# Turning the second pass over a layer's end chunks around, keeping their taps, and leaving GpSimd's products out of eight iterations

## The chip, the cores and the metric

The kernel runs on one core of a Trainium2 chip. The metric is the device time in microseconds (us) of one execution. The kernel before has a median of 3023.64 us in 3 runs (3022.08 to 3026.47).

## What is computed

Four layers work on an image batch x of 4 x 32 x 32 x 16 (batch, rows, columns, channels). Each of the first three normalises x by groups and computes, for every output position ij of the 32 x 32, a 3 x 3 convolution of the whole image with taps of its own, a rectifier of the difference to the image, and a weighted sum over the image:

```
first = jnp.einsum('ijpq,bpqc->bijc', M2, inputs)
K = jnp.transpose(G, (2, 3, 4, 0, 1, 5)).reshape(kh, kw, c, h * w * f)
shifted = lax.conv_general_dilated(inputs, K, window_strides=(1, 1), padding='SAME', ...)
diff = jax.nn.relu(inputs[:, :, :, None, None, :] - shifted)
second = jnp.einsum('ijpq,bpqijc->bijc', W2, diff)
return first - L * second          # and x = x + that
```

The fourth layer is a filter whose impulse response comes from a quotient of transforms. The change doesn't touch its code.

## The kernel before, in words

**Blocks and iterations.** A layer's 1024 positions times 16 channels are 128 blks of 128 rows. One iteration (`iteration`) takes one blk and one batch: TensorE (PE) convolves the whole image (1024 pixels) with the blk's taps into PSUM. Batches 0 and 2 go through `direct` (L637, 10 matmul records in an iteration), batches 1 and 3 through `shared` (L656 and L676, 22 records), which computes part of the sum once for two pixels. ScalarE (ACT) copies that part out of PSUM (L664), and VectorE (DVE) adds it (L684). Then the result is clipped at zero, multiplied by the weights W of the blk and summed over the pixels. DVE does that in one instruction (L725), or ACT clips it into SBUF (L705), GpSimd (POOL) multiplies (L706, here "a product"), and ACT sums (L711). Which way is taken, `by_pool` decides.

**Chunks and their tiles.** Four blks are a chunk; chunks are numbered through the three layers, 32 in each. A chunk needs three things:
- four of the taps, a tile f of 512 KB, loaded by `load_f` (L497) on SyncE's queue (SP) and corrected by one POOL instruction (`minus_mid`, L489). Three buffers in turn.
- the other taps, a tile g. `other_taps` prepares them once for each chunk: it loads E on SP (L525), then POOL makes two sums and a split of them in steps (L489, L530, L534, L536) and stores the pieces to DRAM (gd, L539). `beside_products` spreads the steps over iterations without a product. `piece_loads` fetches them with a broadcast in two DMAs of 768 KB on SP (g<-gd, L554), once the store is noted. Two buffers in turn.
- W for two blks, 1 MB, loaded by `w_loads` on SP (L601). Six buffers in turn.

**The order.** In each layer five jobs follow each other. Job 0 takes the first 12 blks for one pair of batches, job 1 the same 12 blks for the other pair, job 2 the middle 104 blks for all four batches, jobs 3 and 4 the last 12 blks for pair (0, 1), then for pair (2, 3). A pair job has 24 iterations, job 2 has 416. The pairs are (0, 2) and (1, 3) in layer 0, so job 1 there is `shared` alone, and (0, 1) and (2, 3) after it. So a pair's sums are complete while the other pair still has 24 iterations to go, and its next image can be made beside these. Each of jobs 0, 1, 3 and 4 goes through its three chunks from the lowest up, so each chunk is loaded for each pair.

**Behind a pair's end.** `conv_layer` adds the pair's sums to x on DVE (L764) and starts `make_image`: group norm (statistics on DVE, L150 to L180, sums over partitions by PE, L130), centring and scaling (L332, L1077 in the last layer), then `store_image` (pieces on ACT, POOL and DVE, then img<-ys and img<-ye on SP) and `load_image` (f<-img and n<-img, half on SP and half on POOL). PE, DVE, ACT, POOL and SP each work strictly through the order in which the program issued to them.

**Who sets the order.** It is written out by the program itself: a counter now["at"] counts iterations, and every load is a generator that waits for a count. `step` advances them all after each iteration. F of a use u is due at begin[u] - 30, or when use u - 2 begins; g of a use at begin[u] - 12, or when use u - 1 begins, which is eight iterations ahead in a pair job. E of a chunk is planned backwards from that (`ready`: 20 iterations earlier, 14 apart) and forwards through `done`; the very first chunk to be prepared may start at iteration 3, others 8 behind their load. W waits while an image is being stored and loaded (now["image"]).

Of the kernel before, what the change touches and what calls it, by code (L numbers as in the profile page):

```python
# [15 lines left out]
P = 128  # L16
B, C, S = 4, 16, 32
NBLK = 128
# [19 lines left out]
def conv_stack_kernel(ctx, tc, x, M, W, first_w, first_f, first_g, F, E, h0, coef, cst, dft, idp, idq, out):  # L38
# [4 lines left out]
    work = ctx.enter_context(tc.tile_pool(name="work", bufs=1))  # L43
    small = ctx.enter_context(tc.tile_pool(name="small", bufs=2))
    imp = ctx.enter_context(tc.tile_pool(name="image", bufs=1))
    wp = ctx.enter_context(tc.tile_pool(name="wp", bufs=6))
    gs = ctx.enter_context(tc.tile_pool(name="gs", bufs=3))
    gn = ctx.enter_context(tc.tile_pool(name="gn", bufs=2))
    ge = ctx.enter_context(tc.tile_pool(name="ge", bufs=1))
    er = ctx.enter_context(tc.tile_pool(name="er", bufs=2))  # L50
    rp = ctx.enter_context(tc.tile_pool(name="rp", bufs=2))
# [39 lines left out]
    for layer in range(3):  # L91
        firsts = [FIRST, tuple(b for b in range(B) if b not in FIRST)] if layer == 0 else [(0, 1), (2, 3)]
        blks = start[layer]
        passes += [(blks[0], pair) for pair in firsts] + [(blks[1], (0, 1, 2, 3))]
        passes += [(blks[2], pair) for pair in ((0, 1), (2, 3))]
    order, uses, w_first, w_last = [], [], {}, {}
    for blks, batches in passes:
        for blk in blks:
            if blk % GC == 0:
                uses.append([blk // GC, len(order), any(SHARED[b] for b in batches)])  # L100
            w_first.setdefault(blk // 2, len(order))
            order += [(blk, b, len(uses) - 1) for b in batches]
            w_last[blk // 2] = len(order)
    begin = [use[1] for use in uses] + [len(order)]
    now = {"at": 0, "image": 0}

    def until(at):
        while now["at"] < at:
            yield
# [81 lines left out]

    def first_images(nine, g9):

        gn0 = taps_tile().rearrange("p d u s n -> p (d u s n)")
        for u in range(3):
            gt[u] = gn0[:, bass.ts(u, GC * P)]
        rlo = st.tile([P, B], F32, name="rlo")
        ims_of = lambda b: ims[0, b]

# [26 lines left out]

        def first_lo(u, r):
            part = g9[u]
            lo = gt[u][r : r + 32]
            nc.vector.tensor_tensor(lo, part[r : r + 32], lo.bitcast(F32), ALU.subtract)  # L230

        def first_taps(u):
            nc.scalar.copy(gt[u], g9[u])

        all_sums = []

# [196 lines left out]
    def first_term(layer, xt):  # L433

        ft = work.tile([P, 2, 8, S], F32, tag="ft", name="ft")
        with tc.tile_pool(name="mp", bufs=4) as mp:
            mts = [load_m(mp.tile([P, 2 * 512], F32, tag="mt", name="mt"), layer, 0)]
            yield

            yt = work.tile([P, 8, B, C], F32, tag="yt", name="yt")  # L440
            for b in range(B):
                nc.vector.transpose(yt[:, :, b, :], yc[b // 2][:, b % 2, :])
            for pm in range(1, 4):
                mts.append(load_m(mp.tile([P, 2 * 512], F32, tag="mt", name="mt"), layer, pm))
                yield

            for pm in range(4, 8):
                if pm % 2 == 0:
                    while not w_free():
                        yield  # L450
                    wt = w_tile(None)
                mts.append(load_m(wt[:, pm % 2], layer, pm))
                yield
            for _ in range(4):
                yield
            pf = small_psum()
            for k, mt in enumerate(mts):
                for h in range(2):
                    nc.tensor.matmul(  # L459
                        pf[64 * h : 64 * h + 64],  # L460
                        lhsT=yt[:, k].rearrange("k b c -> k (b c)"),
                        rhs=mt[:, bass.ts(h, 512)],
                        start=(k == 0),
                        stop=(k == len(mts) - 1),
                    )
            ring[:] = [last or now["at"] for last in ring]
            nc.scalar.copy(ft, pf.rearrange("k (cc p q) -> k cc p q", cc=2, p=8))
            yield

        fv = fd.rearrange("(p c) b h cc q -> h cc b c p q", p=8)  # L470
        for h in range(2):
            for b in range(B):
                for cc in range(2):
                    at = 64 * h + C * b
                    nc.gpsimd.dma_start(out=fv[h, cc, b], in_=ft[at : at + C, cc])
            yield
        xf = work.tile([P, B, NBLK], F32, tag="ft", name="xf")
        nc.gpsimd.dma_start(
            out=xf.rearrange("p b n -> p (b n)"), in_=fd.rearrange("p b h cc q -> p (b h cc q)")
        )  # L480
        yield
        xr = work.tile([P, B, NBLK], F32, tag="xr", name="xr")
        nc.gpsimd.tensor_tensor(xr, xt, xf, ALU.add)
        return xr

    fours, gt = {}, {}

    def minus_mid(v, m, engine=nc.gpsimd):
        engine.tensor_tensor(  # L489
            v, v, m.unsqueeze(1).to_broadcast([v.shape[0], v.shape[1], C]), ALU.subtract  # L490
        )

    def load_f(u):
        f = gs.tile([P, 2, GC * P], F32, tag="f", name="f")
        fours[u] = f
        layer, ch = divmod(uses[u][0], NBLK // GC)
        nc.sync.dma_start(out=f.rearrange("r k n -> r (k n)"), in_=F[layer][ch])  # L497

    def four_taps(u):

        at = max(begin[u] - 30, begin[u - 2] if u > 2 else 0)
        if u > 1:
            yield from until(at)
            load_f(u)
        yield from until(min(max(at + 8, begin[u] - 16), begin[u] - 2) if u > 1 else 3)
        minus_mid(fours[u][:, 1].rearrange("r (n f) -> r n f", f=C), mid)

    need = {}
    for u, (q, _, _) in enumerate(uses[3:], 3):
        need.setdefault(q, max(begin[u - 1], begin[u] - 12))  # L510

    stored = set()

    def beside_products(n):
        for _ in range(n):
            yield
            while by_pool(*order[now["at"] - 1][:2]):
                yield

    def other_taps(q, at):  # L520
# [18 lines left out]
            nc.gpsimd.dma_start(out=gd[q % len(gd)][k], in_=t.rearrange("r s n -> r (s n)").bitcast(F32))  # L539
        stored.add(q)  # L540

    def taps_tile():
        return gn.tile([P, 3, 2, 2, 2 * P], F32R, tag="g", name="g")

    def piece_loads(u):

        q, first, _ = uses[u]
        yield from until(max(begin[u - 1], first - 12))
        while q not in stored:
            yield  # L550
        gt[u] = t = taps_tile()
        src = gd[q % len(gd)].rearrange("k (c d) x -> (k c) (d x)", d=6)
        for half in range(2):
            nc.sync.dma_start(  # L554
# [4 lines left out]
    def taps_of(u, blk, half, dys, slot=1):  # L559
        rows = slice(64 * half, 64 * half + 64)  # L560
        if u < 3:
            return gt[u][rows, bass.ts(blk % GC, P)]
        v, blk = divmod(blk % GC, 2)
        return gt[u][rows, dys[half], v, slot, bass.ts(blk, P)]

    tasks = []
    done, ready = [-8, -8], {}
    qs = sorted(need, key=need.get)
    for q in reversed(qs):
        ready[q] = max(min(need[q] - 20, ready.get(q + 1, need[q]) - 14), 0)  # L570
    for q in qs:
        load = max(0, done[-2] + 8, ready[q] - 20)
        at = load, max(ready[q], done[-1] + 1, load + (8 if q else 3))
        done.append(at[1] + 6)
        tasks.append((load, other_taps(q, at)))
    tasks += [(begin[u] - 30, four_taps(u)) for u in range(1, len(uses))]
    tasks += [(begin[u] - 12, piece_loads(u)) for u in range(3, len(uses))]
    tasks = [task for _, task in sorted(tasks, key=lambda task: task[0])]

    wts, ring = [], []  # L580

    def w_tile(last):
        ring.append(last)
        return wp.tile([P, 2, S * S], F32, tag="w", name="w")

    def w_free():
        return len(ring) < 6 or ring[-6] is not None and ring[-6] <= now["at"]

    def load_w(parts=1):

# [13 lines left out]
    def w_loads():  # L604
        while len(wts) < len(w_first):
            k = len(wts)
            yield from until(w_first[k] - (24 if k > 5 else 10))
            while not w_free() or now["image"]:
                yield
            list(load_w())  # L610

# [10 lines left out]
    def direct(layer, u, blk, b):  # L622


        pt = pair_psum()
        f = fours[u]
        at = bass.ts(blk % GC, P)
        im, ninth = ims[layer, b]
        for k, t in enumerate((im[:, :, 0], im[:, :, 1], ninth)):
# [16 lines left out]
    def shared(layer, u, blk, b):  # L646


        f = fours[u]
        at = bass.ts(blk % GC, P)  # L650
        fi, ni = ims[layer, b]
        both = pair_psum()[:, :, :256]
# [38 lines left out]

    sums_due = []

    def by_pool(blk, b):
        if END <= blk % NBLK < NBLK - END:
            return b == 2
        if blk < END:
            return b == 1
        return not SHARED[b] and blk % 2 == 0

    def by_gpsimd(pt, blk, to):
        while len(sums_due) > 1:
            one_sum()
# [13 lines left out]
    def iteration(layer, acc):  # L717
        blk, b, u = order[now["at"]]
        assert blk // NBLK == layer
        pt = (shared if SHARED[b] else direct)(layer, u, blk, b)  # L720
        if by_pool(blk, b):
            by_gpsimd(pt, blk, acc[b // 2][:, b % 2, blk % NBLK : blk % NBLK + 1])
            return
        junk = junkp.tile([P, S * S], F32, tag="junk", name="junk")
# [208 lines left out]
    with tc.tile_pool(name="st", bufs=1) as st:  # L933
# [10 lines left out]
        first_part = 4 * P + 2 * NCH  # L944
        coefs = st.tile([P, coef.shape[1]], F32, name="coefs")
        nc.sync.dma_start(out=coefs[:, :first_part], in_=coef[:, :first_part])
        load_f(0)
        ab = coefs[:, : 2 * P]
        ones = coefs[:, 4 * P : first_part].rearrange("p (ch r) -> p ch r", r=2)
        soon_at = [2 * P] + [first_part + 2 * P * ch for ch in range(SOON - 1)]  # L950
# [9 lines left out]
        nc.sync.dma_start(out=coefs[:, first_part:], in_=coef[:, first_part:])  # L960
        list(load_w(2))
        load_first(1)
        load_f(1)
        nc.sync.dma_start(out=g9[1], in_=first_taps(1))
        first_images(nine, g9)
        for _ in range(2):
# [165 lines left out]
    for n, slot in enumerate(then):  # L1132
# [3 lines left out]
        if n == 3:  # L1136
# [5 lines left out]
            for a in range(2):  # L1142
                for i in range(2):
                    nc.gpsimd.dma_start(out=sd[:, a, :, i], in_=side[64 * i : 64 * i + 64, a])
            both = gs.tile([P, 2, GC * P], F32, tag="f", name="both").rearrange("p n m -> p (n m)")
            nc.gpsimd.dma_start(out=both, in_=sd.rearrange("q a b i f -> (q a b) (i f)"))
            bank_of[3] = small_psum()
        run(slot)
# [161 lines left out]
```

## Time and profile before

| what | us |
|---|---|
| median of the runs | 3023.64 |
| the profiled execution | 3019.91 |
| its span | 3018.1 |
| PE busy | 2901.1 (96%) |
| DVE busy | 2407.4 (80%) |
| POOL busy, ACT busy | 1681.5, 1236.7 |
| the DMA queue of SP | 493.58 MB, 71.7% of 16 engines' span |

The jobs in the trace, each from its first matmul to the next job's first:

| layer | job 0 | job 1 | job 2 | job 3 | job 4 |
|---|---|---|---|---|---|
| 0, start | 12.9 | 66.1 | 131.7 | 909.8 | 953.6 |
| 0, took | 53.1 | 65.6 | 778.2 | 43.8 | 54.1 |
| 1, start | 1007.7 | 1073.7 | 1123.9 | 1886.2 | 1929.7 |
| 1, took | 66.1 | 50.1 | 762.3 | 43.5 | 54.0 |
| 2, start | 1983.6 | 2048.5 | 2099.8 | 2861.3 | 2904.9 |
| 2, took | 64.9 | 51.3 | 761.6 | 43.5 | 52.9 |

How the views are read. The slices divide the span by 40 (75 us each); a digit is the busy share in tenths. A row of a timeline has start, duration, engine, line, operation, tiles and shapes, and in brackets how long the engine sat idle before it and what it waited for. A row of the windows has the stretch and its length, then the busy us (and instructions) of PE, its weight load, DVE, ACT and POOL, the granted clock of PE, the busy share of the DMA engines, and GB/s. The chain of waits follows the work that ended last, backwards; a piece has its start, its duration and what it was. Iterations are numbered from 0 to 1535; layer 1 begins at 512, layer 2 at 1024, a layer's job 1 24 later, its job 4 488 later.

### The profile page before, as it was taken

The numbers are of one execution on the slowest core, as the hardware profiler recorded it, in microseconds if no ns is written. First come the engines' busy times: TensorE is split into PE (matmuls) and PEld (weight loads), VectorE is DVE, ScalarE is ACT, GpSimd is POOL, SyncE is SP. The second block draws the span as 40 slices with busy tenths as digits, with TensorE's granted clock in tenths as the row PEclk, the third lists the DMA queues.
The fourth block names the chain that finished last, engine by engine and source line by source line (L and its number), as shares of the span: only waits on it lengthen the run. The fifth ranks groups of instructions, "written<-read, shape, count | busy, mean of one in ns | idle before, by whom it ended". The sixth has DMA issues, their size and how long they took to land. (4 is left out here: it accounts for less than half of the span.)

```text
span 3018.1 us, 62888 instructions
## 1 busy us (share of the span) xinstructions
PE 2901.1 (96%) x25492; PEld 2387.1 (79%) x25492; DVE 2407.4 (80%) x3255; ACT 1236.7 (41%) x2003; POOL 1681.5 (56%) x1450
## 2 busy tenths in 40 slices
PE   7799999999999799999999999979999999999998
PEld 4687778888887578788888888757878888888874
DVE  6787878888888678788888888867878888888883
ACT  2543444444444334344444444433434444444431
POOL 4757767545555555655455555546464555545531
PEclk9999999999999999999999999999999999999999
DMA  9698677767687999777677777799987878877864
GB/s 270 161 232 192 156 174 193 165 162 177 167 186 178 223 210 234 173 170 171 164 178 165 176 166 182 185 220 213 222 187 177 181 181 177 195 166 175 182 144 82
DMA packets 108952, 552.22 MB, mean 183 GB/s; under 512 B 19576, under 2 KB 27960, under 8 KB 69112
## 3 DMA queue, kind: packets, MB, share of 16 engines
q1 hardware_dynamic: 87664, 493.58, 71.7%
q0 software_dynamic: 17808, 47.40, 5.7%
q10 hardware_dynamic: 3192, 7.23, 1.1%
q8 instruction: 202, 3.31, 0.5%
q14 instruction: 86, 0.70, 0.1%
HBM read 501.52 MB, written 46.61 MB: 182 GB/s over the span
## 5 line engine op out<-in xcount | busy, mean ns | idle before, releaser
L706 POOL TENSOR_TENSOR r<-r,w 128x1024 f32<-128x1024 f32 x384 | 909.3, 2368 | 1165.9 <-ACT r L705 1150.3
L637 PE MATMUL pt<-f,f 64*128 64x512 f32 x6144 | 1526.3, 592 | 15.0 <-PE pt L676 6.0
L725 DVE SCALAR_TENSOR_TENSOR junk<-pt,w 128x1024 f32<-128x1024 f32 x1152 | 1410.4, 1224 | 97.6 <-PE pt L637 35.0
L684 DVE TENSOR_TENSOR pt<-pt,both_sb 128x1024 f32<-128x1024 f32 x768 | 945.1, 1231 | 453.0 <-PE pt L676 383.8
L676 PE MATMUL pt<-f,f 64*128 64x256 f32 x6144 | 1044.5, 379 | 26.1 <-ACT r L705 16.1
L676 PE MATMUL pt<-n,g 64*128 64x256 f32 x6144 | 1030.8, 371 | 0.0
L637 PEld LDWEIGHTS pt<-f,f 64*128 64x128 f32 x6144 | 746.5, 187 | 251.5 <-issue 99.3
L705 ACT ACTIVATE r<-pt 128x1024 f32<-128x1024 f32 x384 | 393.6, 1025 | 1038.5 <-PE pt L637 1009.6
L676 PEld LDWEIGHTS pt<-n,g 64*128 64x128 f32 x6144 | 772.8, 188 | 7.8
L637 PE MATMUL pt<-n,g 64*128 64x480 f32 x1536 | 679.6, 780 | 34.8 <-issue 21.5
L664 ACT COPY both_sb<-pt 128x512 f32<-128x512 f32 x768 | 446.6, 583 | 571.2 <-PE pt L656 558.9
L676 PEld LDWEIGHTS pt<-f,f 64*128 64x128 f32 x6144 | 614.6, 187 | 30.4 <-ACT r L705 18.2
L656 PEld LDWEIGHTS pt<-n,g 64*128 64x128 f32 x4608 | 478.0, 187 | 117.7 <-issue 45.8
L656 PE MATMUL pt<-n,g 64*128 64x256 f32 x4608 | 477.3, 279 | 10.5 <-DMA g<-gd 8.7
L711 ACT ACTIVATE r<-r 128x1024 f32<-128x1024 f32 x384 | 410.6, 1069 | 20.9 <-POOL r L706 20.8
L637 PEld LDWEIGHTS pt<-n,g 64*128 64x128 f32 x1536 | 221.6, 188 | 151.9 <-issue 84.2
L489 POOL TENSOR_TENSOR f<-f,cs 128x512 f32<-128x512 f32 x114 | 145.9, 1280 | 22.2 <-DMA f<-in_F_dram 21.7
L530 POOL TENSOR_TENSOR raw<-raw 96x256 f32<-96x256 f32 x192 | 139.3, 726 | 7.7
L536 POOL TENSOR_TENSOR raw<-raw,hi 96x512 fp32r<-96x512 f32 x96 | 122.8, 1279 | 1.4
L725 DVE DVE_READ_ACCUMULATOR junk<-pt,w 128x1 f32 x1152 | 95.9, 83 | 0.0
L711 ACT ACTIVATION_READ_ACCUMULATOR r<-r 128x1 f32 x384 | 77.7, 202 | 0.0
L489 POOL TENSOR_TENSOR raw<-raw,cs 96x256 f32<-96x256 f32 x96 | 70.0, 729 | 7.7 <-DMA raw<-in_E_dram 7.6
(133 smaller groups left out, 558.2 us busy)
## 6 DMA issues: line engine op xcount, KB each, us to landing
w<-in_W_dram SPq DMA_DIRECT2D x188, 1024.0 KB, 14.9
g<-gd SPq DMA_DIRECT2D x222, 768.0 KB, 11.6
f<-in_F_dram SPq DMA_DIRECT2D x114, 512.0 KB, 4.9
raw<-in_E_dram SPq DMA_DIRECT2D x96, 288.0 KB, 3.5
gd<-hi POOLq DMA_DIRECT2D x96, 192.0 KB, 7.3
gd<-raw POOLq DMA_DIRECT2D x96, 192.0 KB, 7.3
mt<-in_M_dram SPq DMA_DIRECT2D x12, 512.0 KB, 19.8
w<-in_M_dram SPq DMA_DIRECT2D x12, 512.0 KB, 21.2
```

The source lines that it names most:

```text
L489: engine.tensor_tensor(v, v, m.unsqueeze(1).to_broadcast([v.shape[0], v.shape[1], C]), ALU.subtract)
L530: nc.gpsimd.tensor_tensor(raw[:, 0], raw[:, 0], raw[:, k], ALU.add)
L536: nc.gpsimd.tensor_tensor(lo, both, hi.bitcast(F32), ALU.subtract)
L637: nc.tensor.matmul(pt[:, half, px], lhsT=taps_of(u, blk, half, (0, 2)) if k == 2 else f[rows, k, at], rhs=rhs, start=k == 0, stop=k == 2,)
L656: nc.tensor.matmul(both[:, half], lhsT=taps_of(u, blk, half, (dy, dy), 0), rhs=ni[rows, dy : dy + 4, 2], start=dy == 0, stop=dy == 2,)
L664: nc.scalar.copy(sb, both)
L676: nc.tensor.matmul(pt[:, half].rearrange("p (r k m) -> p k r m", k=2, m=16)[:, k], lhsT=w, rhs=rhs, start=k == j == 0, stop=k == 1 and j == 2,
L684: nc.vector.tensor_tensor(v, v, sb.rearrange("p h (r m) -> p (h r) m", m=16).unsqueeze(2).to_broadcast([P, 32, 2, 16]), ALU.add,)
L705: nc.scalar.activation(r, pt.rearrange("p h m -> p (h m)"), AF.Relu, scale=-1.0)
L706: nc.gpsimd.tensor_tensor(r, r, wts[blk // 2][:, blk % 2, :], ALU.mult)
L711: nc.scalar.activation(r, r, AF.Copy, scale=-1.0, accum_out=to)
L725: nc.vector.scalar_tensor_tensor(junk, pt.rearrange("p h m -> p (h m)"), 0.0, wts[blk // 2][:, blk % 2, :], ALU.min, ALU.mult, accum_out=a ...
```

## The change

In jobs 1 and 4 the three chunks are taken from the last down; inside a chunk the blks go up as before. The tiles f and g are given to slots by a plan made beforehand: a chunk that still lies in a slot is not loaded again, and a new one takes the slot whose chunk is needed latest, or was used longest ago. W takes the slot that came free first. `by_pool` is replaced by a list `pooled`, which is the same but for "rest": in the first four blks of job 4 of every layer and of job 0 of layers 1 and 2 (eight iterations each) there is no product, which takes out ten, and `beside_products` passes over these iterations too. E is planned 32 iterations ahead of need in place of 20. The chunk that is prepared first is now chunk 2, so the short start of 3 iterations, which is for chunk 0, applies to none. A W load that is needed within six iterations no longer waits for an image. What the tiles hold and what is computed stays.

```
-    wp = ctx.enter_context(tc.tile_pool(name="wp", bufs=6))
-    gs = ctx.enter_context(tc.tile_pool(name="gs", bufs=3))
-    gn = ctx.enter_context(tc.tile_pool(name="gn", bufs=2))
+    wp = ctx.enter_context(tc.tile_pool(name="wp", bufs=1))
+    gs = ctx.enter_context(tc.tile_pool(name="gs", bufs=1))
+    gn = ctx.enter_context(tc.tile_pool(name="gn", bufs=1))
...
-        passes += [(blks[0], pair) for pair in firsts] + [(blks[1], (0, 1, 2, 3))]
-        passes += [(blks[2], pair) for pair in ((0, 1), (2, 3))]
+        back = [[blk for at in reversed(part[::GC]) for blk in range(at, at + GC)] for part in blks]
+        passes += [(blks[0], firsts[0]), (back[0], firsts[1]), (blks[1], (0, 1, 2, 3))]
+        passes += [(blks[2], (0, 1)), (back[2], (2, 3))]
...
+                rest = k < 4 and (job == 4 or layer > 0 and job == 0)
+                quiet.append(rest)
+                if len(batches) == 4:
+                    pooled.append(b == 2)
+                elif n < 2:
+                    pooled.append(b == 1)
+                else:
+                    pooled.append(not (SHARED[b] or rest or blk % 2))
...
+    def plan(held, first):
+
+        loads, n = [], len(held)
+        for u in range(first, len(uses)):
+            q = uses[u][0]
+            slot = next((k for k, h in enumerate(held) if h and h[0] == q), None)
+            if slot is None:
+                again = lambda h: next((v for v in range(u, len(uses)) if uses[v][0] == h[0]), len(uses))
+                slot = max(range(n), key=lambda k: (2 * len(uses), 0) if not held[k] else (again(held[k]), -held[k][1]))
+                free = begin[held[slot][1] + 1] if held[slot] else 0
+                loads.append((u, q, slot, free))
+                held[slot] = [q, u]
+            held[slot][1] = u
+        return loads
+
+    f_plan, g_plan = plan([None] * 3, 0), plan([None, [-1, 2]], 3)
...
-        at = max(begin[u] - 30, begin[u - 2] if u > 2 else 0)
+        at = max(begin[u] - 30, free)
...
-            while by_pool(*order[now["at"] - 1][:2]):
+            while pooled[now["at"] - 1] or quiet[now["at"] - 1]:
                 yield
...
-        yield from until(max(begin[u - 1], first - 12))
+        yield from until(max(free, begin[u] - 12))
...
     for q in reversed(qs):
-        ready[q] = max(min(need[q] - 20, ready.get(q + 1, need[q]) - 14), 0)
+        ready[q] = last = max(min(need[q] - 32, last - 14), 0)
     for q in qs:
         load = max(0, done[-2] + 8, ready[q] - 20)
         at = load, max(ready[q], done[-1] + 1, load + (8 if q else 3))
...
-    def w_free():
-        return len(ring) < 6 or ring[-6] is not None and ring[-6] <= now["at"]
+    def w_free():
+        return any(last is not None and last <= now["at"] for last in ring)
...
-            while not w_free() or now["image"]:
+            while not w_free() or now["image"] and now["at"] < w_first[k] - 6:
                 yield
...
-        if by_pool(blk, b):
+        if pooled[now["at"]]:
```

## The prediction

> **What bounds the kernel now.** First the page's slices: TensorE (PE) is above 90% in most of them, and falls behind at the very start, twice in the middle and at the end.
>
> ```profile
> PE   7799999999999799999999999979999999999998
> ...
> DMA  9698677767687999777677777799987878877864
> ```
>
> Where the row reads 9, PE is the bound, and nothing in this change makes a matmul cheaper. So I cut the trace into the 15 jobs of the order (the table ahead), by counting matmuls: 10 for a direct iteration, 22 for a shared one. An undisturbed pair job takes 43.5 us (job 3: 43.81, 43.52, 43.52). Over that stand: layer 0's jobs 0 and 1 with 9.6 and 22.1, job 4 with 10.6, 10.4 and 9.4, job 0 of layers 1 and 2 with 22.5 and 21.4, their job 1 with 6.6 and 7.7. The change touches only these. Next the busy times of job 4's first eight iterations in layers 0 and 2, and of job 0's in layer 1:
>
> ```profile
> 953.60:977.90 24.30, 17.55 (x139) 13.15 (x135) 20.31 (x36) 6.73 (x15) 11.25 (x15) 0.93 0.60 146
> 1007.70:1044.65 36.95, 20.16 (x146) 14.72 (x144) 18.68 (x39) 9.55 (x21) 11.71 (x13) 0.82 1.02 233
> 2904.90:2926.90 22.00, 16.81 (x139) 12.34 (x135) 19.74 (x38) 5.90 (x11) 6.26 (x4) 0.92 0.51 117
> ```
>
> (Length; PE, weight load, DVE, ACT, POOL; clock; DMA share; GB/s.) Eight iterations want 14.5 us. In job 4 DVE fills 84% and 90% of the time, DMA little over half: DVE sets the pace. At the layer's start DMA is full (1.02): transfers set it. The timelines of DVE and POOL say what DVE is full of:
>
> ```profile
> 956.80 3.37 DVE L764 TENSOR_TENSOR x<-xr,acc 128x256 f32<-128x256 f32 x1
> ...
> 970.87 2.65 DVE L332 TENSOR_SCALAR y<-x,both,rstd 128x128 f32<-128x128 f32 x2
> ...
> 1011.20 0.43 DVE L764 TENSOR_TENSOR x<-xr,acc 128x256 f32<-128x256 f32 x1 [0.42 <-ACT r L711]
> ```
>
> ```profile
> 957.53 2.35 POOL L706 TENSOR_TENSOR r<-r,w 128x1024 f32<-128x1024 f32 x1
> ...
> 971.03 2.40 POOL L706 TENSOR_TENSOR r<-r,w 128x1024 f32<-128x1024 f32 x1 [10.17 <-ACT r L705]
> ```
>
> The same L764 takes 0.43 alone and 3.37 beside a GpSimd product, and ends with it (960.2 against 959.9). L332 does likewise. In layer 2 other instructions are hit: L116 1.72 for 0.17, L179 2.23 for 0.16. Last, PE's timeline at the start of layer 1, and the chain of waits before job 1 of layer 2:
>
> ```profile
> 1007.70 1.91 PE L637 MATMUL pt<-f,f 64*128 64x512 f32 x8
> 1019.60 0.73 PE L637 MATMUL pt<-n,g 64*128 64x480 f32 x1 [9.99 <-issue]
> 1023.56 0.74 PE L637 MATMUL pt<-n,g 64*128 64x480 f32 x1 [3.23 <-DMA g<-gd]
> ```
>
> ```profile
> 2025.09 13.06 DMA f<-img
> ...
> 2043.05 12.05 DMA g<-gd
> ...
> 2055.29 0.73 PE pt L637
> ```
>
> Both stalls end with a g tile. The second is the reload of chunk 64 for the second pair, queued behind the pair's image; the image itself was in at about 2043, job 1 could have begun at 2048.5.
>
> **The change, part by part.** Read off order and planner: F loads 114 to 96, g loads 111 to 101 (two DMAs each), SP's queue 38 DMAs shorter, 25 MB of 552 less; 18 of the L489 f subtractions (1.28 us, POOL) gone; GpSimd products 384 to 374. PE's work is the same, so only the stalls count.
>
> *Job 1 of layers 1 and 2.* It opens with the chunk that job 0 ended with: its F and g are in SBUF. The reload goes from eight iterations ahead of the job to iteration 8 of it, for iteration 16, with F ahead of it on SP and no image loads. It then has 14.5 us; the page's median for g is 11.6, and such eight-iteration reloads held in job 1 before. What is next late is the image: last pieces at about 1068 and 2043, PE there at 1073.7 and 2048.5, so 5.5 us of cover, and an F load less ahead of it. Gain 6.6 + 7.7 = 14.3; I take 14.
>
> *Job 4 of layers 0 and 1.* Two products go to DVE (1.23 + 0.08 each), and 2 x (1.03 + 1.27) leave ACT. On DVE's path from L764 to the end of L332: blocked time off 3.37 - 0.43 = 2.94 and 2.65 - 0.60 = 2.05 (0.60 is the like pair L1077 undisturbed), two products on, -2.62, and two idle gaps behind PE's wait for L117 (0.68 and 0.62) close: 2.94 + 2.05 - 2.62 + 1.30 = 3.7. The image store moves up as much, and PE with it. Here a rule speaks against the change: the Trainium skill, Perfetto Trace Analysis, "Optimizing Scalar/DVE Operations", says that where DVE is saturated, moving work off it to Scalar or GPSIMD may pay (and warns that those two share a read port). DVE is nearly saturated here; by the rule the ten products cost 10 x 1.31 = 13 us; by the rows five windows win some 11. I go by the rows, which are these very instructions.
>
> *Job 0 of layers 1 and 2.* The 16 us stall at its first iteration stays: chunk 32's g is issued at iteration 504 as before, behind two W tiles and F, after an image store and a g load of equal size (chunk 29 for 31); the loads saved here lie ahead of 966, when the queue ran empty. It moves up with the store (3.7). Against it: the E preparation is due 12 iterations earlier, so E of chunk 35 (288 KB) now stands ahead of that g: 0.29 MB at 233 GB/s, -1.3. Its first product falls into DVE's idle 14.7 us, the second costs 1.31 and frees L332 by 2.05: +0.7. Each boundary: 3.7 - 1.3 + 0.7 = 3.1; two, 6.2. If the clock of that queue is not the store, 3.7 is swallowed by a longer stall: bound 0.
>
> *Job 4 of layer 2.* Blocked: 1.55 + 2.07 + 0.66 (L1077, beside an f subtraction that is dropped) = 4.3, less 2.62 = 1.7, and of 1.42 of DVE's gaps some; walking the eight iterations I get 2.2.
>
> *Layer 0, job 1.* PE ended iteration 23 at 60.6 and waited for g of chunk 0 until 69.9, iteration 24 was done at 73.4, 62.5 without. That load stood behind the last image's loads on SP. Now chunk 2 comes first: its preparation starts at iteration 8 (the 3 for chunk 0 becomes 8), lies on POOL ahead of the last image's loads, its store at about 46, its g on SP ahead of them, at 50.5. 1.5 MB at the 214 GB/s of 40 to 60 land at 58 to 59, the image half behind it at 62: stall 0 to 1.5 instead of 10.9. Gain 10. But the 8 shifts the chain: chunk 3's store moves from iteration 40 to 44, on POOL from 116.3 to behind iteration 42's product (125.7), +9.4. Its g landed at 132.05 for a job 2 that began at 131.65: no cover. It now moves alone (8 us, not 11.7): on the old scale 138, PE wants it at 133. Stall 5, of which some 2 were DVE backlog in the next iterations anyway: -3. Net 7, ends 0 and 10.
>
> *At nothing:* tiles by slot (the same six, three and two buffers, free at the same iterations), the steps of E moved within the middle (POOL 56% busy), W loads let through at six iterations (the image flag is up in iterations 494 to 498, the deadline is 510), steps held through quiet iterations (chunk 34's store at 500, wanted at 520). If POOL's cover were gone, each step is under 1.6 us.
>
> Sum: 14 + 2 x 3.1 + 2.2 + 7 = 29.4. The profiled execution took 3019.9 for a span of 3018.1; the median is 3023.6, 0.1% more, so I subtract from the median: 2994.
>
> **The rivals.**
> - *Only the reloads pay* (0.2): the layer's start absorbs what job 4 wins, and chunk 3 eats layer 0's gain. 14 + 2.2 = 16: 3007. For it: DMA at 1.02, no cover at 131.65. Against: the store that starts the queue's work moves too.
> - *The full queue shortens too* (0.08): with 25 MB less, the 16 us stalls lose 5 to 7 each: 2982. Against: the bytes saved are not in those 30 us.
> - *The reloads are hidden anyway, the image ends the wait* (0.06): then job 1 gains nothing. With job 4's gain swallowed at the layer's start and chunk 3 at its full 9, 2.2 + 1 are left: 3020. Against: the image was in 5.5 us before PE, both times.
> - *DVE becomes the bound behind a pair's end* (0.06): the port is held by E's steps (0.7 to 1.5 us) as L764 comes, no block ends, and each added product costs twice over, because PE waits in order for the group norm's sums. Five windows at 5.2 are 26, plus 2.6 for E, less 21: 8 slower, 3031. It decides from 4.2 us a window on (21 / 5). For it: 84 to 90% DVE. Against: chunk 34's first steps can run at 952 to 955, before L764 at 956.8.
>
> **How the numbers follow.** The forecast has 0.6: 2994, by itself 2985 to 3003 (layer 0 from 0 to 10, the boundaries from 0 to 3.7 each). With the first two rivals the range is 2980 to 3011. About 0.2%, 6 us, is what a measurement of this kernel can tell from no change: faster 0.88, same 0.06, slower 0.06.
>
> **What would show it.** Right: L764 at 0.4 to 0.5 in all six places; job 1 of layers 1 and 2 at 44 us; no g reload in the chain of waits there; 16 us still lost at the first iteration of layers 1 and 2, ended by g; job 4 at 50 to 51; PE in layer 0 going on at 61 to 63, and a new wait for g of chunk 3 at the start of job 2. Wrong: an image wait opening job 1, job 4 at 54 or more with DVE full, or a wait of PE for w or f that was not there.

## The result

The changed kernel takes 3027.1 us in the median of 20 runs (3022.3 to 3033.9), the kernel before 3023.5 beside it (3019.1 to 3031.8): a ratio of 1.0012, interval 1.0005 to 1.0020. That is no gain; the forecast was 2994. Most of what it promised is in the trace; about as much, and a little more, was lost, the most of it in places where it expected nothing.

The jobs of the changed kernel's trace, and what each took against before:

| layer | job 0 | job 1 | job 2 | job 3 | job 4 |
|---|---|---|---|---|---|
| 0 | 47.5 (-5.6) | 65.3 (-0.3) | 798.5 (+20.3) | 43.5 (-0.3) | 52.0 (-2.0) |
| 1 | 69.4 (+3.4) | 43.4 (-6.7) | 763.7 (+1.4) | 43.5 | 52.0 (-1.9) |
| 2 | 67.9 (+3.1) | 43.4 (-7.8) | 769.5 (+7.9) | 43.5 | 49.1 (-3.8) |

The differences add up to +7.6, and the two profiled spans are 3026.6 and 3018.1, 8.5 apart. (The medians are only 3.6 apart: the profiled execution of before lies 3.6 under its median, that of the changed kernel 1.3 over its own.) The largest entry is job 2 of layer 0, where nothing was forecast. The slices of the page show it too:

```profile
PE   8798999999999799999999999979999999999998
```

The fourth digit of PE, 227 to 303 us, is an 8 where it was a 9. The other views answer to those of before. First the windows of job 4's first eight iterations in layers 0 and 2, and of job 0's in layer 1 (the second row):

```profile
967.84:987.54 19.70, 16.06 (x138) 12.09 (x134) 17.28 (x41) 3.68 (x11) 2.56 (x7) 1.00 0.22 54
1019.88:1051.87 31.99, 19.13 (x137) 14.41 (x133) 16.98 (x38) 3.59 (x11) 3.78 (x8) 0.79 1.02 224
2916.36:2936.70 20.34, 17.57 (x141) 12.28 (x139) 18.30 (x42) 3.06 (x7) 0.00 (x0) 0.92 0.00 1
```

Eight iterations are 4.6, 3.0 and 2.2 us shorter than before. (For layer 1 the row of before takes in a ninth iteration, which began at 1042.64; in layer 2 the row here goes 0.5 beyond the eighth.) DVE still fills 88 to 90% of job 4's; the DMA share in the first has gone from 0.60 to 0.22, in the third from 0.51 to 0.00. (Job 0 of layer 1 is 3.0 shorter in its first eight iterations and 3.4 longer as a whole: what it loses lies behind them, in the iterations from 520 to 535.) The two rows of DVE that used to end together with a GpSimd product:

```profile
970.96 0.42 DVE L787 TENSOR_TENSOR x<-xr,acc 128x256 f32<-128x256 f32 x1
...
982.53 0.60 DVE L360 TENSOR_SCALAR y<-x,both,rstd 128x128 f32<-128x128 f32 x2
```

These are L764 and L332 of before, 0.42 for 3.37 and 0.60 for 2.65. L787 takes 0.42 or 0.43 in all six places. And PE's timeline at the start of layer 1, where PE waits 11 us (twice for g of chunk 32; 13.2 before), a stall that was forecast to stay:

```profile
1029.46 0.73 PE L667 MATMUL pt<-n,g 64*128 64x480 f32 x1 [7.67 <-DMA g<-gd]
1033.56 0.74 PE L667 MATMUL pt<-n,g 64*128 64x480 f32 x1 [3.37 <-DMA g<-gd]
```

Job 1 of layers 1 and 2 has no wait at its start any more. So most of what the change was traced to win is won. Now the losses. I counted for each iteration by how much PE is later than before (the lag). Where an iteration is given a time below, it is its length, from its first matmul to that of the next; undisturbed, a direct one takes 1.9 us and a shared one 1.7. In layer 0 the lag jumps in two places: at iteration 48, the start of job 2, and from 122 to 131.

**Iteration 48.** PE's timeline there:

```profile
129.43 0.49 PE L667 MATMUL pt<-n,g 64*128 64x480 f32 x1 [1.71 <-DMA g<-gd]
134.09 0.76 PE L667 MATMUL pt<-n,g 64*128 64x480 f32 x1 [4.17 <-DMA g<-gd]
```

It is the wait for g of chunk 3 that was forecast, but the lag goes from -5.8 to +0.8 here: 6.6 lost, 3 forecast. In the 4 us after the wait (134 to 138) PE was granted half of its clock (0.50).

**Iterations 122 to 131.** The lag grows from 0.8 to 14.5. PE waits for no load there. These are the rows of POOL before the change, in the same stretch:

```profile
251.88 4.20 POOL L475 DMA_DIRECT2D fd<-ft  x8 [0.29 <-DMA fd<-ft]
...
260.72 0.62 POOL L478 DMA_DIRECT2D xf<-fd  x1
...
273.76 1.28 POOL L483 TENSOR_TENSOR xr<-x,xf 128x512 f32<-128x512 f32 x1 [6.41 <-DMA xf<-fd]
```

The layer's first term is written to DRAM in two groups of eight small stores (fd<-ft), read back in another order (xf<-fd) and added to x, all of it on POOL. After the change:

```profile
247.28 4.21 POOL L503 DMA_DIRECT2D fd<-ft  x8
251.49 0.62 POOL L563 CAST hi<-raw 96x512 fp32r<-96x512 f32 x1
252.19 1.29 POOL L565 TENSOR_TENSOR raw<-raw,hi 96x512 fp32r<-96x512 f32 x1
253.44 2.36 POOL L729 TENSOR_TENSOR r<-r,w 128x1024 f32<-128x1024 f32 x1
...
256.80 4.19 POOL L503 DMA_DIRECT2D fd<-ft  x8
...
274.73 0.62 POOL L506 DMA_DIRECT2D xf<-fd  x1 [10.12 <-DMA fd<-ft]
...
285.08 1.27 POOL L511 TENSOR_TENSOR xr<-x,xf 128x512 f32<-128x512 f32 x1 [6.67 <-DMA xf<-fd]
```

E's steps for chunk 9 (L563, L565 and their neighbours) used to run at iterations 112 to 117. Planned 32 ahead they run at 103 to 108, in front of the second group of stores, which leaves at 256.80 in place of 251.88. Those 5 us matter because of SP: from 257.58 to 259.99 it issues F (512 KB), g (1536), E (288) and W (1024). The first two of the eight stores are down by 261.0; the other six take 6.8 to 13.7 us for 16 KB each, and the last lands at 274.17 (before: 257.3). POOL stands 10.12 us in front of the read (not at all before), then 6.67 in front of the addition (6.41 before). So the addition is done 11.3 us later than before, and the product of iteration 122 is queued behind that. ACT waits for that product, then DVE and PE for ACT:

```profile
290.85 1.06 ACT L734 ACTIVATE r<-r 128x1024 f32<-128x1024 f32 x1 [10.06 <-POOL r L729]
```

In layer 2 the same stores enter the chain that ended last, where before the change there is no such piece:

```profile
2229.13 14.69 DMA fd<-ft
...
2244.64 7.93 DMA xf<-fd
...
2256.07 2.32 POOL r L729
```

It costs 7.9 us there (iterations 1146 to 1152) and 2.1 in layer 1 (638). The rest of the loss lies behind the pairs' ends: the iterations 508 and 1020 (2.5 each), 532 to 534 (7) and 1044 (3). The chain shows one of these in layer 2; L453 is the last half of an image load, on POOL:

```profile
2042.69 1.04 POOL n L453 x2
...
2046.01 0.75 POOL raw L559
...
2049.55 2.36 POOL r L729
```

POOL comes out of the image load and has steps of E (L559, L563) to do before the product of iteration 1044.

### The profile page after: what moved, and what is told of

Same layout as the page of the kernel before. It is cut to its first block, busy times and chain, and to the rows that moved or that the text cites. A ratio compares the mean times of both kernels' runs of the same rounds, so it can differ in the third digit from the quotient of the medians.

```text
span 3026.6 us, 62755 instructions
## 1 busy us (share of the span) xinstructions
PE 2905.8 (96%) x25492; PEld 2381.0 (79%) x25492; DVE 2399.7 (79%) x3275; ACT 1216.2 (40%) x1973; POOL 1635.3 (54%) x1422
## 5 line engine op out<-in xcount | busy, mean ns | idle before, releaser
L729 POOL TENSOR_TENSOR r<-r,w 128x1024 f32<-128x1024 f32 x374 | 885.2, 2367 | 1117.4 <-ACT r L728 1074.6
L728 ACT ACTIVATE r<-pt 128x1024 f32<-128x1024 f32 x374 | 383.5, 1025 | 974.3 <-PE pt L667 933.7
L734 ACT ACTIVATE r<-r 128x1024 f32<-128x1024 f32 x374 | 399.9, 1069 | 66.8 <-POOL r L729 66.8
L559 POOL TENSOR_TENSOR raw<-raw 96x256 f32<-96x256 f32 x192 | 139.5, 727 | 7.6
L517 POOL TENSOR_TENSOR f<-f,cs 128x512 f32<-128x512 f32 x96 | 122.9, 1281 | 24.1 <-DMA f<-in_F_dram 23.8
L565 POOL TENSOR_TENSOR raw<-raw,hi 96x512 fp32r<-96x512 f32 x96 | 122.9, 1280 | 1.8
```

The source lines that it names most:

```text
L517: engine.tensor_tensor(v, v, m.unsqueeze(1).to_broadcast([v.shape[0], v.shape[1], C]), ALU.subtract)
L559: nc.gpsimd.tensor_tensor(raw[:, 0], raw[:, 0], raw[:, k], ALU.add)
L565: nc.gpsimd.tensor_tensor(lo, both, hi.bitcast(F32), ALU.subtract)
L728: nc.scalar.activation(r, pt.rearrange("p h m -> p (h m)"), AF.Relu, scale=-1.0)
L729: nc.gpsimd.tensor_tensor(r, r, wts[blk // 2][:, blk % 2, :], ALU.mult)
L734: nc.scalar.activation(r, r, AF.Copy, scale=-1.0, accum_out=to)
```

## The experiments

**The theory:** the loss comes from one number, E planned 32 iterations ahead in place of 20. It moves steps on POOL's queue in front of the first term's stores (in the middle) and in front of products (behind a pair's end). **A second part:** chunk 3 is late because chunk 2 no longer gets the short start. **Rivals:** turning the order around is itself the cause, or the missing products are.

**20 again.** In the changed kernel:

```
-        ready[q] = last = max(min(need[q] - 32, last - 14), 0)
+        ready[q] = last = max(min(need[q] - 20, last - 14), 0)
```

> The changed kernel with one number put back: E of a chunk is planned 20 iterations ahead of need, not 32. Theory A (the advance of the E preparation is the loss: on GpSimd's queue it pushes the first term's stores into the load burst of iterations 112 to 116, and it sits behind the image loads ahead of the products): the stalls at iterations 122 to 131 (13.7 us), 638 (2.1), 1146 to 1152 (7.9), 508, 1020, 532 to 534 and 1044 (some 13) go: 2988 to 2992. Theory B (turning the chunks around and keeping tiles in slots disturbs the loads themselves): these stalls stay, 3020 to 3030. Theory C (taking products off GpSimd costs it): likewise 3020 to 3030. The wait for g of chunk 3 at iteration 48 (some 6 us) stays by all three.

Measured: 2994.6 us, ratio to before 0.9907 (0.9891 to 0.9922), 2.6 above theory A's range. The waits at 122 to 131, 638 and 1146 are gone; iteration 48 still takes 8.1. The 32 costs 32.5 us between the medians: more than the whole forecast gain.

**The short start back,** for the chunk that is now prepared first:

```
-        at = load, max(ready[q], done[-1] + 1, load + (8 if q else 3))
+        at = load, max(ready[q], done[-1] + 1, load + (8 if q != qs[0] else 3))
```

> The changed kernel with the short start (3 iterations in place of 8) given to the chunk that is now prepared first, chunk 2. If chunk 3 is late because the chain of preparations begins 5 iterations later, its store moves back from iteration 44 to 40 and the stall of 6.4 us at iteration 48 goes, the rest stays: 3019 to 3023. If its g is late because DMA is full there, the stall stays: 3026 to 3029.

Measured: 3013.8, ratio 0.9965 (0.9950 to 0.9979). That is 13 won in all, more than was expected of the one wait. Iteration 48 waits no longer: 6.1 in the traces. Iteration 24 is 5.0 shorter, which was not expected; there the changed kernel waits for a part of the image:

```profile
64.07 0.98 PE L686 MATMUL pt<-n,g 64*128 64x256 f32 x5 [3.24 <-DMA n<-img]
```

So jobs 0 and 1 of layer 0 take 107.8 in place of 112.8. And some 7 are in the middle of layer 0, where of iterations 122 to 131 only 127 and 131 are longer than before the change, at 6.3 and 5.0 (2.6 and 3.6 before). The rows of POOL say why:

```profile
244.32 4.21 POOL L503 DMA_DIRECT2D fd<-ft  x8
...
252.98 0.62 POOL L506 DMA_DIRECT2D xf<-fd  x1 [0.85 <-DMA fd<-ft]
```

With the earlier start the planner puts chunk 9's steps at 100 to 105; the second group of stores leaves before most of SP's loads (F at 246.45 is the first large one) and has landed when POOL comes to the read: 0.85 us of waiting, not 10.12. The run was not made to test that, but it says the same. In layers 1 and 2 the loss stays (638 takes 4.5, 1150 takes 6.2).

**Both repairs.**

> The changed kernel with both: 20 iterations and the short start for chunk 2. If the two losses are separate, they add: 2981 to 2986, and the gains of the forecast (14 from the reloads, about 6 at the pairs' ends, 10 in layer 0) are all there. If the shift of layer 0 brings a new collision, 2988 to 2995.

Measured: 2984.2, ratio 0.9872 (0.9857 to 0.9887). It beats both kernels. Jobs 0 and 1 of layer 0 take 108.3 (before 118.7), job 4 of each layer 50.8, 50.9, 48.6.

**32 in the old kernel,** nothing else:

```
-        ready[q] = max(min(need[q] - 20, ready.get(q + 1, need[q]) - 14), 0)
+        ready[q] = max(min(need[q] - 32, ready.get(q + 1, need[q]) - 14), 0)
```

> The kernel before with only the 32 in place of 20. Theory A: it loses by itself what the changed kernel lost in the middle jobs: the stall at iterations 122 to 131, 638 and 1146 appears, some 10 to 25 us, 3034 to 3048. Theories B and C: the 32 is harmless, 3020 to 3027.

Measured: 3040.7, ratio 1.0047 (1.0031 to 1.0063): 14 slower than before by the ratio, 17 between the medians. Iterations 126 and 127 take 5.7 and 7.1, 638 takes 4.4, 1150 takes 5.0, POOL waits 7.25 in front of xf and 6.01 in front of xr; the three jobs 2 are 9.5, 2.6 and 6.0 longer than before. The first iteration of layers 1 and 2 grows from 16.0 to 19.0 and 18.7. So neither the turned order nor the missing products are needed for the loss.

**The stores on another queue.** The changed kernel with the first term's stores issued by ACT:

```
-                    nc.gpsimd.dma_start(out=fv[h, cc, b], in_=ft[at : at + C, cc])
+                    nc.scalar.dma_start(out=fv[h, cc, b], in_=ft[at : at + C, cc])
```

> The changed kernel with the first term's sixteen stores (fd<-ft) issued from ScalarE's queue in place of GpSimd's. Theory A1 (E's steps, moved ahead of these stores on GpSimd's queue, make them leave with the load burst of iteration 112, they land 15 us late, and GpSimd stands behind xf and xr): they leave early again, and the stalls at iterations 122 to 131, 638 and 1146 go (13.7 + 2.1 + 7.9): 3000 to 3007. Theory A2 (E's steps take GpSimd's own time there from the products): the stalls stay, 3020 to 3030.

Measured: 3028.4, ratio to before 1.0011 (1.0003 to 1.0018). A miss as to the time. POOL's wait in front of xf is gone, as are those of PE at 122, 638 and 1146, while E's steps stand where they stood and SP still issues F, g, E and W in one burst (from 264.62): so it was not these steps' own time (A2). But now ACT stands in the stores. First SP's rows, then ACT's (SPq and ACTq are their sequencers):

```profile
236.44 0.55 SPq L631 DMA_DIRECT2D w<-in_W_dram  x1
237.08 0.54 SPq L554 DMA_DIRECT2D raw<-in_E_dram  x1
```

```profile
247.66 5.89 ACTq L503 DMA_DIRECT2D fd<-ft  x3
253.64 0.58 ACT L694 COPY both_sb<-pt 128x512 f32<-128x512 f32 x1 [8.84 <-DMA fd<-ft]
```

The merged row is three issues of 0.31 us each, at 247.66, 249.54 and 253.24. Each waits for a semaphore (numbers 103, 104 and 107 in the trace) by which SP's loads W, E and a second W (issued at 236.44, 237.08 and 237.67) report their landing, and follows that landing (247.63, 249.52, 253.22) by 0.02 to 0.03 us: the program gives the DMAs of SP and ACT the same eight semaphores in turn. So ACT stood for loads that have nothing to do with its stores. Iterations 107 and 108 take 7.8 and 2.3, 619 and 620 take 7.0 and 3.7, 1131 and 1132 take 7.0 and 3.3. The place was right; moving the stores to an engine that is on PE's path only moved the wait.

**20 for chunk 9 of each layer alone.**

```
-        ready[q] = last = max(min(need[q] - 32, last - 14), 0)
+        ready[q] = last = max(min(need[q] - (20 if q % 32 == 9 else 32), last - 14), 0)
```

> The changed kernel with 20 iterations for one chunk of each layer alone, the tenth (prepared at iteration 112 again, not 103), and 32 for all others. Theory A1 and A2: the stalls at 122 to 131, 638 and 1146 go, those at 508, 532 and 1044 stay: 3000 to 3008. If all chunks' advance matters alike, 3020 to 3027.

Measured: 3026.1, ratio 1.0011 (1.0002 to 1.0020): nothing. The edit was idle. Chunk 10 stays at 116, and `last - 14` holds chunk 9 at 102; POOL's order between 245 and 257 us is the same as without it. So it tells nothing on the theory, and I widened it.

**20 for chunks 9 to 14,** so that the chain of 14 lets chunk 9 go back to 112:

```
-        ready[q] = last = max(min(need[q] - 32, last - 14), 0)
+        ready[q] = last = max(min(need[q] - (20 if 8 < q % 32 < 15 else 32), last - 14), 0)
```

> The changed kernel, with E planned 20 ahead again for chunks 9 to 14 of each layer alone (those prepared beside the first term); all others stay at 32. Theory (the earlier steps get in front of the first term's f stores on POOL's queue): in layer 0 the steps of chunk 9 fall at iterations 112 to 117 again, behind the second eight f stores of iteration 108; the waits at iterations 122 to 131 (13.7 us), 638 (2.1) and 1146 to 1152 (7.9) go, those at 508, 532, 1020 and 1044 stay: 3027 - 24 = 3003, between 3000 and 3008. Rival (planning 32 ahead fills POOL and SP in the whole middle, the place is chance): the stall moves to another chunk, 3018 to 3027.

Measured: 3003.0, ratio 0.9925 (0.9908 to 0.9942), as the theory had it: 24 us by the medians (26 by the ratios) lie in this one collision. In the traces the three jobs 2 are 14.7, 2.1 and 7.4 shorter than in the changed kernel. POOL, beside the rows above:

```profile
252.66 4.20 POOL L503 DMA_DIRECT2D fd<-ft  x8 [0.45 <-DMA fd<-ft]
...
261.35 0.62 POOL L506 DMA_DIRECT2D xf<-fd  x1
```

Stores that leave 4.1 us earlier let the read leave 13.4 us earlier. (With them E and the second W leave SP later, at 278.05 and 278.46 in place of 259.32 and 264.98; but with the stores on ACT, where that burst stayed whole, these waits were gone too.) The waits at 508 (3.5), 532 (5.5) and 1044 (5.1) stay.

**The steps not held through the quiet iterations,** with 32 kept:

```
-            while pooled[now["at"] - 1] or quiet[now["at"] - 1]:
+            while pooled[now["at"] - 1]:
```

> The changed kernel, without holding E's steps through the eight quiet iterations (they are only kept off iterations with a product, as before the change). Theory (steps that are held end up on POOL behind the image loads and ahead of the next products): chunk 34's steps go back to iterations 489 to 491, chunk 35's to 519 to 523, and the waits at iterations 508, 1020 (2.5 each), 532 to 534 (7) and 1044 (3) shrink: 3027 - 15 = 3012; the steps may hold the port beside L787 or L360, at most 1.5 us each, so up to 3016. Rival (the waits behind a pair's end come from the image loads on POOL alone, whatever else stands there): no change, 3024 to 3029.

Measured: 3023.7, ratio 0.9997 (0.9989 to 1.0006): 3.4 us better than the changed kernel, hardly clear of the noise; 15 were expected. The waits at 508 and 1020 did go, and job 4 of layers 0 and 1 is 2.6 shorter in each. But iteration 512 grew from 13.9 to 18.6: PE comes earlier to a g that is not earlier. And 532 and 1044 are still at 4.0 and 3.0. Holding the steps is therefore a small part; the layer's start swallows what is won ahead of it.

**The same with both repairs.**

> The changed kernel with both repairs (20 ahead, short start of 3 for the first chunk prepared) and without the holding of E's steps through quiet iterations: as with both repairs alone (2984), if 20 ahead has already taken the steps away from the image loads; 2980 to 2988. If holding still costs there, the store of chunk 33 leaves at iteration 489 in place of 498, its g is earlier for iteration 520 (3.4 and 2.8 us now), and the time is 2978 to 2981.

Measured: 2983.6, ratio 0.9857 (0.9843 to 0.9872), 0.6 us from the repairs alone. Job 4 gets 0.9 and 1.4 us shorter, the next job 0 takes 2.3 and 1.7 more. With 20 ahead the holding costs nothing that can be measured.

**The products back,** with both repairs:

```
-                rest = k < 4 and (job == 4 or layer > 0 and job == 0)
+                rest = False
```

> The run with 20 iterations and the short start, with the ten GpSimd products put back and no quiet iterations. If the products' hold on the port is what job 4 won, L764 or its neighbours take 2 to 3 us again and job 4 goes from 51, 51 and 49 to 53 or 54: 2991 to 2998. If the dropped f subtractions alone had freed the port, 2982 to 2987. If the quiet iterations cost more than they bring in job 0, faster than 2982.

Measured: 2991.7, ratio 0.9890 (0.9875 to 0.9905). So leaving the ten products out is worth 7.4 us by the medians, 5.4 by the ratios (all four runs lie above the four of both repairs); in the traces the three jobs 4 differ by 3.2 in all and the two jobs 0 by 5.3. And one reading of mine falls. Here is POOL with the products back, at the start of job 4 in layer 0, and then DVE:

```profile
945.60 1.28 POOL L565 TENSOR_TENSOR raw<-raw,hi 96x512 fp32r<-96x512 f32 x1
947.54 2.35 POOL L729 TENSOR_TENSOR r<-r,w 128x1024 f32<-128x1024 f32 x1 [0.66 <-ACT r L728]
```

```profile
947.23 0.42 DVE L787 TENSOR_TENSOR x<-xr,acc 128x256 f32<-128x256 f32 x1
...
948.21 1.70 DVE L144 CAST pieces<-st 128x8 fp32r<-128x8 f32 x1
```

The product is there, and L787 still takes 0.42. In the kernel before, POOL at 955 to 960 ran:

```profile
955.07 1.28 POOL L489 TENSOR_TENSOR f<-f,cs 128x512 f32<-128x512 f32 x1
956.30 1.29 POOL L536 TENSOR_TENSOR raw<-raw,hi 96x512 fp32r<-96x512 f32 x1
957.53 2.35 POOL L706 TENSOR_TENSOR r<-r,w 128x1024 f32<-128x1024 f32 x1
```

L764 came at 956.80, in the middle of L536, and got through only after the product that followed without a gap. The f subtraction ahead of it belonged to a reload that the new order saves; without it POOL is 1.3 us earlier and has a gap of 0.66 us in which L787 fits. The block of the product then falls on the next DVE instruction, a cast of 8 elements a row, 1.70 us. (Undisturbed it takes 0.17.) So of the 2.94 us that I gave to the missing products at L764, they bring 1.53, and the other 1.41 come from the missing f reload, as I read these rows; no run put that reload back alone. The row of L764 falls to 0.42 either way, so that sign of the forecast did not tell the two apart. L360 is 2.65 with the products and 0.60 without: that one was read rightly.

**g ahead of W at the layer's start,** with both repairs; W is held from iteration 495 to 504:

```
-            while not w_free() or now["image"] and now["at"] < w_first[k] - 6:
+            while not w_free() or (now["image"] or 494 < now["at"] % 512 < 505) and now["at"] < w_first[k] - 6:
```

> The run with 20 iterations and the short start, in which W loads are also held in iterations 495 to 504 of each layer, so that g of the next layer's first chunk stands ahead of two W tiles on SP. If the first iteration of layers 1 and 2 waits for the bytes ahead of that g, 2 MB less at 243 GB/s bring it 8 us earlier each: stalls of 12.7 and 14.4 go to 4 to 7, and the run to 2966 to 2974, or 2974 to 2980 if W is then late instead. If the image's own loads end that wait, nothing changes: 2982 to 2987.

Measured: 2993.2, ratio 0.9891 (0.9871 to 0.9910), 9 slower than the repairs alone by the medians, 6 by the ratios, and in none of the ranges named. Iteration 512 falls from 12.7 to 7.9 and 1024 from 14.4 to 6.6, but eight iterations later PE waits for the next g: iteration 520 takes 13.9 (3.4 without) and 1032 takes 14.9 (2.8):

```profile
1031.42 0.77 PE L667 MATMUL pt<-n,g 64*128 64x480 f32 x1 [7.83 <-DMA g<-gd]
```

The second half of that g was issued at 1002.79 and landed at 1035.49, with the DMA engines full (share 1.02 from 1003 to 1036). With the queue that full, the new order only chose who waits.

## Why the prediction was wrong

- *"At nothing: ... the steps of E moved within the middle (POOL 56% busy)"* is the step that failed. Steps that cost nothing themselves changed what POOL issues when. Planned 20 ahead again for chunks 9 to 14 only, they give back 24.1 us (3027.1 to 3003.0); for all chunks, 32.5. *"If POOL's cover were gone, each step is under 1.6 us"* priced the step, not what is queued behind it: eight stores, a read, an addition, a product.
- *Chunk 3, "Stall 5 ... : -3".* The mechanism held, the size did not: PE waited 5.9, and 6.6 were lost, because the 2 us of later backlog that I set against it were not given back.
- *Layer 0, job 1, "Gain 10".* The gain was 5.8. Iteration 24, the first shared one, was done at 67.6, not at 62.5 to 64: PE waited 3.24 for a part of the image (the row under "The short start back"). The image's loads left SP behind chunk 2's g, which was issued at 51.89, not at 50.5; and from 64.0 to 67.6 PE was granted half of its clock (0.50). With the short start back, g is issued at 46.80, PE does not wait, and iteration 24 is done at 62.5. So the 8 in place of the 3, which the forecast charged to chunk 3 alone, cost twice: net -0.8 in place of +7. With both repairs jobs 0 and 1 of layer 0 gain 10.4.
- *Job 0 of layers 1 and 2.* The forecast made them 0.6 longer each (1.3 for E of chunk 35 ahead of g, less 0.7); they are 3.4 and 3.1 longer. With 32 at the boundaries only, they take 5.8 and 5.0 more than with 20 throughout (68.4 and 69.3 against 62.6 and 64.3). In which part it is E's bytes and in which the steps on POOL was not separated.
- *Job 4.* 2.0, 1.9 and 3.8, for 3.7, 3.7 and 2.2. With 20 ahead it is 3.1, 3.3 and 4.3. The sum is 7.7 for 9.6, with 20 ahead 10.7; half of what was put down to L764's product was the f reload's.
- *The rule against the rows.* By the rule of the Trainium skill (Perfetto Trace Analysis, "Optimizing Scalar/DVE Operations") ten products moved to a nearly full DVE were a cost of 13, by the rows five windows won some 11. Measured, with both repairs: a gain of 5 to 7. The rows had the sign right, though part of their 11 was the f subtraction's. The same section warns that GpSimd and DVE share an SBUF read port, so that moving work between those two might not help; it is this half of it that fits here (L360: 2.65 us beside a product, 0.60 without).
- *Job 1 of layers 1 and 2.* 14 forecast, 14.5 measured. The image came in time.
- *The rivals.* That DVE becomes the bound gave 3031, near the time, and is wrong: no block came, job 4 got shorter. That the layer's start swallows what job 4 wins is partly right, by the run without holding. No rival had POOL's order in the middle in it, and of the signs named for being wrong only an image wait opening a job 1 came, and that in layer 0. The large loss came by none of them: PE waited for no w or f, but for ACT.

With both repairs the gains in the traces are 14.5 in the jobs 1 (14 forecast), 10.6 in the jobs 4 (9.6), 10.4 in layer 0 (10 without chunk 3's wait), and 5.0 in the jobs 0 of layers 1 and 2, where without E's advance the forecast comes to 1.4 and leaving out the products alone made 5.3; less 1.7 elsewhere, 38.8 in all. The medians of those runs (3023.2 before) are 39.0 apart.

## What to carry to other kernels

When a plan's lead time is changed, list for every moved step what stands behind it on its engine, DMA issues above all, and what the other queues issue in the next few microseconds. Here a small store that left among large loads in place of just ahead of them landed after 13.7 us in place of 1.8, and everything queued in order behind its reader waited. A change that bundles one number with a reordering should be measured without the number: here the rest of the change was worth 1.3% with the lead time and the short start left as they had been.

## What the runs showed of the hardware

- Eight stores of 16 KB that left POOL while SP's queue moved nothing (252.66 to 256.33, with 20 for chunks 9 to 14) landed 1.8 to 3.4 us after their issue. Of the eight that left among 3360 KB of SP's loads (changed kernel), six took 6.8 to 13.7. The Trainium skill (DMA: Bandwidth & Descriptors, "Queues, rings and completion order") says that a DMA engine takes turns between its queues, one packet at a time; POOL's packets in the changed kernel (384, 0.52 MB from 256 to 275 us) are far smaller than SP's (495, 3.04 MB), which fits, but no run varied the packet size.
- Issuing one of layer 0's sixteen stores cost ACT 0.31 to 0.45 us of its sequencer, with the DMA engines full (share 1.00 from 242 to 247 us) as with a share of 0.37 (254 to 260). What held ACT for 8.84 us were three semaphores that it shares with loads of SP.
- L764, a DVE instruction with two inputs, began twice in the middle of L536 on GpSimd (956.80 and 1932.81 us) and ended 0.3 us after the product that followed without a gap: 3.37 and 3.35 us. Begun in a gap of 0.66 us on GpSimd, it took 0.42.
- After PE had waited it ran for some microseconds at half of its clock: granted 0.50 from 64.0 to 67.6 and from 134 to 138 us, 1.00 before either wait (57 to 60.5, 125 to 129).
